# One odd product in 16 on VectorE, read-out two units behind, projection started one block earlier

## The chip, the cores and the metric

The kernel runs on one core of one Trainium2 chip. The metric is the device time of one execution in microseconds (us); before the change it is 21,916.79 us, the median of 3 runs (21,913.64 to 21,924.9). The engines are named as the profile names them: PE (TensorE), ACT (ScalarE), DVE (VectorE), POOL (GpSimd) and SP (SyncE, which issues the DMAs). PSUM is the accumulator memory, SBUF the working memory.

## What is computed

The input x is 16 images of 64 x 64 pixels with 96 channels, in fp32. Two residual layers follow each other. The first upsamples a group-normalised image, runs a small per-pixel network with a quadratic activation, filters and subsamples. The second, which the change is about, is a selective state-space scan over the pixels in four directions. Its core in the reference:

```python
delta = jax.nn.softplus(dts + dt_bias[None, :, :, None])
def step(h, inps):
    dt, ut, bt, ct = inps
    h = jnp.exp(dt[..., None] * As[None]) * h + (dt * ut)[..., None] * bt[:, :, None, :]
    y = jnp.einsum('bkdn,bkn->bkd', h, ct)
    return (h, y)
_, ys = jax.lax.scan(step, h0, (dT, uT, BT, CT))
...
y = ys[:, 0] + ys[:, 2, :, ::-1] + y_wh
...
y = out_norm_w * (y - mu) * jax.lax.rsqrt(var + EPS) + out_norm_b
y = y * z
```

There are 4,096 pixels in a sequence, 192 channels, 16 states per channel and 4 directions. For each channel and state the recurrence is h = decay * h + drive, with decay = exp(delta * A) and drive = delta * u * B; the result is the sum over states of h * C.

## The kernel before

**Tiling.** The scan is cut into 16 images x 8 steps. A step is 1,024 pixels (T) of one pair of directions: four steps forwards, then four backwards. A step has 6 blocks of two groups of 32 channels each, and a block has 4 units, each of which takes 4 of the 16 states of both groups: 32 channels x 4 states fill 128 partitions. So a step has 24 units, an image 192, and the whole run 3,072. The two groups of a unit are called e = 1 (here: odd) and e = 0 (even).

**One unit n** of the loop (the loop at L833), in the order in which it is issued:
- `recur(n, 1)`: DVE scans the odd group. It reads the decay `da` from PSUM and the drive `b` from SBUF and writes the states over `b` (L740 forwards, L742 backwards).
- `keep`: ACT copies the last column into the tile `new`, as the start of the next step (L748). The last step of a direction keeps nothing.
- `decay(n + 1, 1)`: ACT makes the odd decay of the next unit in PSUM (L725). There are two `da` buffers.
- `read_out(n - 1)`: PE multiplies the states times C of the unit before with `fold_s`, which sums over the 4 states, into the PSUM tile `y` (L764). One `y` tile serves the 4 units of a block; in backward steps it starts from the stored forward part `y0` (L757).
- POOL multiplies the odd states by `ct`, the rows of C, in place (L877), and then runs `drive(n + 2)`, the product of `dtu` and `bt` for both groups of the unit after next (L731). `b` has three buffers.
- `recur(n, 0)`: DVE scans the even group, over `da` in PSUM. DVE multiplies by `ct` from PSUM into `b` (L887), ACT keeps the last column and makes `decay(n + 1, 0)`.
- `store`: when a block's last read-out has been issued, ACT copies `y` out (L775) and a DMA writes it.

**Background work.** Between these, three places per unit (`slot(0)`, `slot(1)`, `slot(2)`; 72 positions a step) take one slice each of other work, written as Python generators that yield at each slice. `project` prepares the next step: it loads u (L634), projects it to `pp` on PE (L640), copies it to `pr` (L643), and for each of 3 channel groups v makes softplus: `s` on PE (L650), `e` and `d` on ACT (L658 to L661), `d` and `s` and `dtu` on DVE (L664 to L672), `delta` on ACT (L674); `dtu` and `delta` go to DRAM (L676, L677) and come back broadcast over partitions (L684). `front` makes the first layer and the convolution of the next image, `finish` the norm and output projection of the image before. A pace is kept: a generator advances while slices done / positions is below the ratio set for it (`SLICES` over 576 for front and finish, `PSLICES` over 59 for project).

**Order and queues.** The order on every engine is the order of issue above (a manual schedule); nothing reorders it. All DMAs go through SP's queue. Waits between engines are semaphores that the framework places from the tiles that are read, written and reused. At the start of a step's last block (unit 20) the projection of the next step is drained and its first `dtu` fetched.

Of the kernel before, what the change touches and what calls it, by code (L numbers as in the profile page):

```python
# [45 lines left out]
F32 = mybir.dt.float32  # L46
# [5 lines left out]
C = 96  # L52
# [19 lines left out]
SLICES = 540  # L72
WAIT = -1
HEAVY = 2
PSLICES = 60
# [3 lines left out]
def tile_two_blocks(  # L79
# [103 lines left out]
    b12 = ctx.enter_context(tc.tile_pool(name="b12", bufs=1))  # L183
# [56 lines left out]
    def front(mi):  # L240
# [72 lines left out]
        for p0 in range(0, UPS, PP):  # L313
# [94 lines left out]
        JS = 44  # L408
        s = [
            b18.tile([UPS, JS, C], F32, name="s0", tag="b18"), b12.tile([UPS, HW - JS, C], F32, name="s1", tag="b12")  # L410
        ]
        for _ in range(2):
            yield
        for i, n, first in [(0, JS // 4, k * JS // 4) for k in range(4)] + [(1, 10, 0), (1, 10, 10)]:
            nc.sync.dma_start(out=s[i][:, first:first + n, :], in_=s_d[:, JS * i + first:JS * i + first + n, :])
            yield
# [4 lines left out]
        for j0 in range(0, HW + 8, 8):  # L421
            if done is not None:
                nc.scalar.activation(
                    x1v[:, :, j0 - 8:j0], done.rearrange("c w h -> c h w"), AF.Identity, bias=shift
                )
            if j0 < HW:
# [5 lines left out]
                for j in range(8):  # L432
                    nc.tensor.matmul(
                        done[:, j, :], lhsT=s[(j0 + j) // JS][:, (j0 + j) % JS, :], rhs=down_s, start=False, stop=True,
                        skip_group_check=True,
                    )
            yield
        yield from parts(made["x1"], x1)
# [167 lines left out]
    def scan():  # L606


        with ExitStack() as es:
            pj = es.enter_context(tc.tile_pool(name="sc_pj", bufs=1))  # L610
            up_ = es.enter_context(tc.tile_pool(name="sc_u", bufs=3))
            cp = es.enter_context(tc.tile_pool(name="sc_bc", bufs=5))
            p3 = es.enter_context(tc.tile_pool(name="sc_3", bufs=3))
            p2 = es.enter_context(tc.tile_pool(name="sc_2", bufs=2))
            yp = es.enter_context(tc.tile_pool(name="sc_y", bufs=1))
            stp = es.enter_context(tc.tile_pool(name="sc_st", bufs=2))
            banks.append(es.enter_context(tc.tile_pool(name="b_ps", bufs=2, space=PSUM)))
# [4 lines left out]
            def project(mi, pair, lc, out):  # L622
# [3 lines left out]
                out["rows"] = rows = dram.tile([2, 2 * NS, T], F32, name="rows")  # L626
                out["delta"] = [dram.tile([128, T], F32, name=f"delta_d{v}") for v in range(3)]
                out["dtu"] = [dram.tile([128, T], F32, name=f"dtu_d{v}") for v in range(3)]
                xs_d = image[mi]["xs"]
                for t in range(0, T, TB):  # L630
                    u = []
                    for v in range(3):
                        uv = up_.tile([128, TB], F32, name="u")
                        nc.sync.dma_start(out=uv, in_=xs_d[v, :, lc * T + t:lc * T + t + TB])  # L634
                        u.append(uv)
                    for _ in range(3):
                        yield
# [3 lines left out]
                    yield  # L641
# [4 lines left out]
                    for i, v in enumerate((0, 2, 1)):  # L646
# [20 lines left out]
                        yield  # L667
# [60 lines left out]
            def drive(n):  # L728
                b = p3.tile([128, 2, T], F32, name="b")
# [14 lines left out]
            def keep(n, e, h):  # L744
                st, bi, j = units[n]
                if st % NT < NT - 1:
                    end = h[:, T - 1:T] if steps[st][1] == 0 else h[:, 0:1]
                    nc.scalar.copy(states[bi][1][:, e, j:j + 1], end)  # L748
# [77 lines left out]
            last = len(units) - 1  # L826
            for n in range(2):
                drive(n)
# [4 lines left out]
            for n, (st, bi, j) in enumerate(units):  # L833
# [184 lines left out]
```

## Time and profile before

| what | us |
|---|---|
| median of 3 runs | 21,916.79 |
| the profiled execution, its own time | 21,910.69 |
| its span, first to last instruction | 21,908.9 |
| first product on POOL starts | 513.35 |
| last product on POOL ends | 21,745.4 |
| DVE busy between 16,000 and 21,000 us | 4,695.32 of 5,000 |
| POOL busy between 16,000 and 21,000 us | 4,928.27 of 5,000 |

The profile lists, for each group of instructions, the source line, engine and operation, the tiles written and read with their shapes, a count, the busy time in us and the mean of one in ns; after a second bar, the time that the engine stood idle just before instructions of the group, and what ended it. A list of waits has, for each pair of lines, the total us, the number of times, and the longest. A timeline has the start and the duration in us, and in brackets the idle time before and its releaser. Durations of neighbours on one engine overlap by up to 0.1 us, so the step from start to start is the better measure of what an instruction costs.

### The profile page before, as it was taken

Reading aid. Unit: us, or ns where it says so; the run is one execution under the profiler, and the core shown is the slowest. Engines: PE = TensorE matmul, PEld = TensorE weight load, DVE = VectorE, ACT = ScalarE, POOL = GpSimd, SP = SyncE. Lnnn points to the kernel's source line nnn. Section 1 sums busy time; section 2 is a strip of 40 time slices with the busy share of each in tenths; the row PEclk is TensorE's granted clock in tenths of the full one; section 3 lists DMA queues with packets and bytes.
Section 4 is the critical chain, followed back from the end, with each engine's and each line's share of the span. In section 5 each row is a group of like instructions: output and inputs, shape, how many; then the busy total and the mean of one; then the engine's idle time right before and its main releaser. Section 6 shows DMA issues by size and latency. Waiting matters only on the chain.

```text
span 21908.9 us, 260666 instructions
## 1 busy us (share of the span) xinstructions
PE 15342.2 (70%) x92844; PEld 6324.7 (29%) x92844; DVE 19849.9 (91%) x12829; ACT 13130.2 (60%) x20854; POOL 20900.4 (95%) x6152
## 2 busy tenths in 40 slices
PE   6766767766777677777767677767777677677745
PEld 4322323232232322324233232322323223242211
DVE  0999999999999999999999999999999999999996
ACT  4665656666565665656656566665656656566543
POOL 0999999999999999999999999999999999999997
PEclk7776777877778777777877778777787877778856
DMA  2555565656656566565655656556565655656654
GB/s 80 190 191 188 193 214 194 209 195 200 205 191 215 189 206 201 192 215 192 207 198 194 214 192 209 196 201 206 193 211 189 210 199 198 206 195 208 210 177 134
DMA packets 1851895, 4276.30 MB, mean 195 GB/s; under 512 B 449118, under 2 KB 548350, under 8 KB 1848542
## 3 DMA queue, kind: packets, MB, share of 16 engines
q1 hardware_dynamic: 1850590, 4259.62, 58.1%
q8 instruction: 731, 11.98, 0.2%
q14 instruction: 574, 4.70, 0.1%
HBM read 3380.58 MB, written 878.18 MB: 194 GB/s over the span
## 4 chain that ended last, share of the span: by engine, by line
DVE 36%; POOL 19%; issue 18%; PE 9%; ACT 9%; DMA 7%; SPq 1%; POOLq 0%; DVEq 0%; ACTq 0%
POOL b L731 10%; POOL b L877 10%; DVE da L742 7%; DVE da L740 7%; DVE b L740 6%; DVE b L742 6%; DVE b L887 4%; ACT da L725 4%; DMA u<-xs_d 2%; DVE s L669 2%; DVE dtu L672 2%; DVE s L668 2%; PE y L764 1%; DMA ct<-rows 1%; PE pp L640 1%
## 5 line engine op out<-in xcount | busy, mean ns | idle before, releaser
L731 POOL TENSOR_TENSOR b<-dtu,bt 128x2048 f32<-128x2048 f32 x3072 | 13984.9, 4552 | 584.6 <-DMA dtu<-dtu_d 522.9
L725 ACT ACTIVATE da<-delta,a_s 128x1024 f32<-128x1024 f32 x6144 | 6853.5, 1116 | 2826.6 <-DVE b L887 1185.9
L877 POOL TENSOR_TENSOR b<-b,ct 128x1024 f32<-128x1024 f32 x3072 | 7309.1, 2379 | 259.8 <-ACT new L748 249.5
L764 PE MATMUL y<-b,fold_s 128*32 128x256 f32 x49152 | 4638.9, 492 | 4107.3 <-DVE b L887 3102.6
L887 DVE TENSOR_TENSOR b<-da,ct 128x1024 f32<-128x1024 f32 x3072 | 3752.6, 1222 | 84.5
L764 PEld LDWEIGHTS y<-b,fold_s 128*32 128x32 f32 x49152 | 1353.3, 126 | 7627.7 <-DVE b L887 4083.3
L740 DVE TENSOR_TENSOR_SCAN da<-da,new,b 128x1024 f32<-128x1024 f32 x1152 | 2694.3, 2339 | 252.3 <-ACT da L725 252.3
L740 DVE TENSOR_TENSOR_SCAN b<-da,new,b 128x1024 f32<-128x1024 f32 x1152 | 2698.0, 2342 | 174.1 <-POOL b L731 166.9
L742 DVE TENSOR_TENSOR_SCAN da<-da,new,b 128x1024 f32<-128x1024 f32 x1152 | 2693.8, 2338 | 172.9 <-ACT da L725 172.7
L742 DVE TENSOR_TENSOR_SCAN b<-da,new,b 128x1024 f32<-128x1024 f32 x1152 | 2697.1, 2341 | 151.6 <-POOL b L731 109.5
L748 ACT COPY new<-da 128x1 f32<-128x1 f32 x2304 | 362.3, 157 | 3028.5 <-DVE b L887 3023.2
L473 PE MATMUL c_ps<-xgp,wtap_s 96*128 96x512 f32 (+1 forms) x4608 | 1817.8, 675 | 168.9 <-ACT row L491 164.1
L650 PE MATMUL s<-pr,dtw_s 128*128 128x512 f32 x1536 | 1120.4, 819 | 557.8 <-ACT delta L674 516.7
L377 PE MATMUL o_ps<-w2c_s,hsq 128*100 128x96 f32 x9600 | 1205.3, 293 | 191.9 <-ACT hsq L348 180.1
L365 PE MATMUL h_ps<-xu,w1t_s 96*128 96x500 f32 x1920 | 1147.6, 700 | 244.2 <-ACT hsq L348 108.6
L748 ACT COPY new<-b 128x1 f32<-128x1 f32 x2304 | 432.6, 188 | 1445.7 <-DVE b L742 740.4
L377 PEld LDWEIGHTS o_ps<-w2c_s,hsq 128*100 128x100 f32 x9600 | 1119.5, 203 | 407.4 <-ACT hsq L348 227.7
L640 PE MATMUL pp<-u,xpt_s 128*128 128x512 f32 x1536 | 903.7, 734 | 224.2 <-DMA u<-xs_d 216.0
L742 DVE TENSOR_TENSOR_SCAN b<-da,b 128x1024 f32<-128x1024 f32 x384 | 876.7, 2283 | 133.2 <-ACT da L725 74.8
L473 PEld LDWEIGHTS c_ps<-xgp,wtap_s 96*128 96x128 f32 (+1 forms) x4608 | 631.9, 182 | 1193.3 <-issue 938.6
L740 DVE TENSOR_TENSOR_SCAN da<-da,b 128x1024 f32<-128x1024 f32 x384 | 875.8, 2281 | 106.9 <-ACT da L725 106.9
L742 DVE TENSOR_TENSOR_SCAN da<-da,b 128x1024 f32<-128x1024 f32 x384 | 876.0, 2281 | 105.0 <-ACT da L725 105.0
(120 smaller groups left out, 18077.1 us busy)
## 6 DMA issues: line engine op xcount, KB each, us to landing
dtu<-dtu_d SPq DMA_DIRECT2D x1536, 512.0 KB
delta<-delta_d SPq DMA_DIRECT2D x1536, 512.0 KB
bt<-rows SPq DMA_DIRECT2D x1024, 512.0 KB
ct<-rows SPq DMA_DIRECT2D x1024, 512.0 KB
u<-xs_d SPq DMA_DIRECT2D x896, 256.0 KB
dtu_d<-dtu SPq DMA_DIRECT2D x768, 256.0 KB
delta_d<-delta SPq DMA_DIRECT2D x768, 256.0 KB
xr<-in_x SPq DMA_DIRECT2D x768, 128.0 KB
```

Of the source, the lines that this page charges most:

```text
L365: nc.tensor.matmul(h_ps[j], lhsT=w1t_s[:, 128 * j:128 * (j + 1)], rhs=xu.rearrange("c p q -> c (p q)"), start=True, stop=True,)
L377: nc.tensor.matmul(o_ps[:, p, :], lhsT=hsq[j][:, UPS * p:UPS * (p + 1)], rhs=w2c_s[:, j, :], start=(j == 0), stop=(j == HB - 1),)
L473: nc.tensor.matmul(c_ps[p:p + n], lhsT=wtap_s[:, tap, 128 * i:128 * i + n], rhs=xgp[:, h0:h0 + 8, dx:dx + HW], start=(tap == 0), stop=(tap ...
L640: nc.tensor.matmul(pp, lhsT=xpt_s[:, pair, v, :], rhs=u[v], start=(v == 0), stop=(v == 2))
L650: nc.tensor.matmul(s, lhsT=dtw_s[:, pair, v, :], rhs=pr, start=True, stop=True)
L725: nc.scalar.activation(da, ops["delta", n // NQ][:, e, :], AF.Exp, scale=a_s[:, k, g, units[n][2]:units[n][2] + 1])
L731: nc.gpsimd.tensor_mul(b, ops["dtu", n // NQ], bt.unsqueeze(1).to_broadcast([128, 2, T]))
L740: nc.vector.tensor_tensor_scan(out, da, b, before, ALU.mult, ALU.add)
L742: nc.vector.tensor_tensor_scan(out[:, ::-1], da[:, ::-1], b[:, ::-1], before, ALU.mult, ALU.add)
L764: nc.tensor.matmul(y[32 * q:32 * q + 32, e, :], lhsT=fold_s, rhs=b[:, e, QT * q:QT * q + QT], start=(pair == 0 and j == 0 and e == 0), sto ...
L877: nc.gpsimd.tensor_mul(h, h, bc[1, r, j])
L887: nc.vector.tensor_mul(bs[n][:, 0, :], h, bc[1, r, j])
```

## The change

- Of every 16 units the last (n % 16 = 15) has its odd states written to PSUM, over `da`, and multiplied by `ct` on DVE instead of POOL. `keep` then copies from PSUM, after the product.
- `read_out` and `store` run two units behind instead of one. `b` has four buffers instead of three. `fetch_y0` is issued at the end of a block for the next one.
- The projection for step k is begun at the last block of step k - 2 (`next_step`) instead of at the start of step k - 1, and paced 71 slices over 72 positions instead of 60 over 59. Two positions instead of one lie after `pp`, after the second `s` on ACT and after `delta`. The first u tiles are fetched four slices ahead, the second ones as soon as a buffer is free (four u buffers instead of three). The DRAM tiles of a step have three buffers.
- In `front`, `s` is loaded into one buffer in two turns of 40 and 24 rows (before: two tiles, 44 and 20), with two slices between neighbouring groups of matmuls. `SLICES` goes from 540 to 550.

```diff
@@ -69,10 +69,11 @@
 NEPS = 1e-5
 BOTH = "natural_log_exp_and_others"
 POS = 3 * 8 * 6 * NQ
-SLICES = 540
+SLICES = 550
+SHARE = 16
 WAIT = -1
 HEAVY = 2
-PSLICES = 60
+PSLICES = 71
 
 
 @with_exitstack
...
@@ -405,14 +405,16 @@
         stow(sd, UPS - 2 * PG)
 
 
-        JS = 44
-        s = [
-            b18.tile([UPS, JS, C], F32, name="s0", tag="b18"), b12.tile([UPS, HW - JS, C], F32, name="s1", tag="b12")
-        ]
+        def fetch_s(first, n):
+            t = b18.tile([UPS, n, C], F32, name="s", tag="b18")
+            for k in range(0, n, 8):
+                nc.sync.dma_start(out=t[:, k:k + 8, :], in_=s_d[:, first + k:first + k + 8, :])
+                yield t, first
+
+        JS = 40
         for _ in range(2):
             yield
-        for i, n, first in [(0, JS // 4, k * JS // 4) for k in range(4)] + [(1, 10, 0), (1, 10, 10)]:
-            nc.sync.dma_start(out=s[i][:, first:first + n, :], in_=s_d[:, JS * i + first:JS * i + first + n, :])
+        for s, s_first in fetch_s(0, JS):
             yield
         yield
         x1 = xt
@@ -423,6 +425,11 @@
                 nc.scalar.activation(
                     x1v[:, :, j0 - 8:j0], done.rearrange("c w h -> c h w"), AF.Identity, bias=shift
                 )
+            if j0 == JS:
+                for s, s_first in fetch_s(JS, HW - JS):
+                    yield
+                for _ in range(2):
+                    yield
             if j0 < HW:
                 done = bank([C, 8, HW], "e_ps")
                 nc.tensor.matmul(
...
@@ -608,12 +617,13 @@
 
         with ExitStack() as es:
             pj = es.enter_context(tc.tile_pool(name="sc_pj", bufs=1))
-            up_ = es.enter_context(tc.tile_pool(name="sc_u", bufs=3))
+            up_ = es.enter_context(tc.tile_pool(name="sc_u", bufs=4))
             cp = es.enter_context(tc.tile_pool(name="sc_bc", bufs=5))
-            p3 = es.enter_context(tc.tile_pool(name="sc_3", bufs=3))
+            p4 = es.enter_context(tc.tile_pool(name="sc_4", bufs=4))
             p2 = es.enter_context(tc.tile_pool(name="sc_2", bufs=2))
             yp = es.enter_context(tc.tile_pool(name="sc_y", bufs=1))
             stp = es.enter_context(tc.tile_pool(name="sc_st", bufs=2))
+            dctx = es.enter_context(tc.tile_pool(name="dctx", bufs=3, space=bass.MemoryType.DRAM))
             banks.append(es.enter_context(tc.tile_pool(name="b_ps", bufs=2, space=PSUM)))
             aps = es.enter_context(tc.tile_pool(name="sc_aps", bufs=2, space=PSUM))
             yps = es.enter_context(tc.tile_pool(name="sc_yps", bufs=1, space=PSUM))
@@ -623,27 +633,32 @@
 
 
 
-                out["rows"] = rows = dram.tile([2, 2 * NS, T], F32, name="rows")
-                out["delta"] = [dram.tile([128, T], F32, name=f"delta_d{v}") for v in range(3)]
-                out["dtu"] = [dram.tile([128, T], F32, name=f"dtu_d{v}") for v in range(3)]
+                out["rows"] = rows = dctx.tile([2, 2 * NS, T], F32, name="rows")
+                out["delta"] = [dctx.tile([128, T], F32, name=f"delta_d{v}") for v in range(3)]
+                out["dtu"] = [dctx.tile([128, T], F32, name=f"dtu_d{v}") for v in range(3)]
                 xs_d = image[mi]["xs"]
+                order = (0, 2, 1)
+
+                def fetch_u(v, t):
+                    uv = up_.tile([128, TB], F32, name="u")
+                    nc.sync.dma_start(out=uv, in_=xs_d[v, :, lc * T + t:lc * T + t + TB])
+                    return uv
+
+                ahead_u = [fetch_u(v, 0) for v in order]
+                for _ in range(4):
+                    yield
                 for t in range(0, T, TB):
-                    u = []
-                    for v in range(3):
-                        uv = up_.tile([128, TB], F32, name="u")
-                        nc.sync.dma_start(out=uv, in_=xs_d[v, :, lc * T + t:lc * T + t + TB])
-                        u.append(uv)
-                    for _ in range(3):
-                        yield
+                    u, ahead_u = dict(zip(order, ahead_u)), []
                     pp = gps.tile([128, TB], F32, name="pp", tag="g")
                     for v in range(3):
                         nc.tensor.matmul(pp, lhsT=xpt_s[:, pair, v, :], rhs=u[v], start=(v == 0), stop=(v == 2))
-                    yield
+                    for _ in range(2):
+                        yield
                     pr = pj.tile([128, TB], F32, name="pr")
                     nc.scalar.activation(pr, pp, AF.Identity, bias=bumps_s)
 
 
-                    for i, v in enumerate((0, 2, 1)):
+                    for i, v in enumerate(order):
                         if i == 0:
                             yield
                         s = gps.tile([128, TB], F32, name="s", tag="g")
@@ -664,7 +679,8 @@
                         nc.vector.scalar_tensor_tensor(d, s, 0.0, d, ALU.max, ALU.add)
                         yield
                         nc.scalar.activation(s, e, AF.Identity, bias=one_s)
-                        yield
+                        for _ in range(2):
+                            yield
                         nc.vector.scalar_tensor_tensor(s, s, -1.0, e, ALU.add, ALU.subtract)
                         nc.vector.tensor_sub(s, d, s)
                         dtu = pj.tile([128, TB], F32, name="dtu")
@@ -672,19 +688,25 @@
                         nc.vector.tensor_mul(dtu, s, u[v])
                         yield
                         nc.scalar.copy(delta, s)
-                        yield
+                        for _ in range(2):
+                            yield
                         nc.sync.dma_start(out=out["dtu"][v][:, t:t + TB], in_=dtu)
                         nc.sync.dma_start(out=out["delta"][v][:, t:t + TB], in_=delta)
+                        if t + TB < T and i < 2:
+                            ahead_u += [fetch_u(k, t + TB) for k in (order[:1], order[1:])[i]]
+
+            def spread(out, what, ctx, bi, e):
+
+                v, s0, r = blocks[bi]
+                nc.sync.dma_start(
+                    out=out,
+                    in_=ctx[what][v][32 * (s0 + e):32 * (s0 + e) + 32, :].unsqueeze(1).to_broadcast([32, NQ, T]),
+                )
 
             def fetch(what, ctx, bi):
-
-                v, s0, r = blocks[bi]
                 t = p2.tile([128, 2, T], F32, name=what)
                 for e in (1, 0):
-                    nc.sync.dma_start(
-                        out=t[:, e, :],
-                        in_=ctx[what][v][32 * (s0 + e):32 * (s0 + e) + 32, :].unsqueeze(1).to_broadcast([32, NQ, T]),
-                    )
+                    spread(t[:, e, :], what, ctx, bi, e)
                 return t
 
             def fetch_bc(ctx, r, j, what):
@@ -726,7 +748,7 @@
                 das[n, e] = da
 
             def drive(n):
-                b = p3.tile([128, 2, T], F32, name="b")
+                b = p4.tile([128, 2, T], F32, name="b")
                 bt = bc[0, blocks[units[n][1]][2], units[n][2]]
                 nc.gpsimd.tensor_mul(b, ops["dtu", n // NQ], bt.unsqueeze(1).to_broadcast([128, 2, T]))
                 bs[n] = b
@@ -741,11 +763,11 @@
                 else:
                     nc.vector.tensor_tensor_scan(out[:, ::-1], da[:, ::-1], b[:, ::-1], before, ALU.mult, ALU.add)
 
-            def keep(n, e, h):
+            def keep(n, e, h, copy):
                 st, bi, j = units[n]
                 if st % NT < NT - 1:
                     end = h[:, T - 1:T] if steps[st][1] == 0 else h[:, 0:1]
-                    nc.scalar.copy(states[bi][1][:, e, j:j + 1], end)
+                    copy(states[bi][1][:, e, j:j + 1], end)
 
             def read_out(n):
                 st, bi, j = units[n]
@@ -824,6 +846,15 @@
                 (ahead_gen if ahead_gen.gen is not None else behind_gen).slot(position)
 
             last = len(units) - 1
+            def next_step(st, mi):
+
+                nonlocal step_gen
+                if st < len(steps):
+                    if steps[st][0] > mi:
+                        ahead_gen.drain()
+                    step_gen = Background(project(*steps[st], ctxs[st]), PSLICES, 3 * per_step)
+
+            next_step(1, 0)
             for n in range(2):
                 drive(n)
             for e in range(2):
@@ -843,10 +874,6 @@
                 elif n % per_image == 2 and mi > 0:
                     behind_gen = Background(finish(mi - 1), SLICES, POS)
                 if j == 0:
-                    if bi == 0 and st + 1 < len(steps):
-                        if steps[st + 1][0] > mi:
-                            ahead_gen.drain()
-                        step_gen = Background(project(*steps[st + 1], ctxs[st + 1]), PSLICES, 59)
                     new = stp.tile([128, 2, NQ], F32, name="new", tag=f"st{bi}")
                     states[bi] = (states[bi][1] if states[bi] else None, new)
 
@@ -857,41 +884,46 @@
                     elif n + NQ <= last:
                         step_gen.drain()
                         ahead = ctxs[st + 1], 0
+                        next_step(st + 2, mi)
                     if ahead:
                         ops["dtu", m + 1] = fetch("dtu", *ahead)
                 elif j == 1:
                     if ahead:
                         ops["delta", m + 1] = fetch("delta", *ahead)
-                    if n + NQ <= last and steps[units[n + NQ - 1][0]][1] == 1:
-                        st2, bi2, _ = units[n + NQ - 1]
-                        y0s[steps[st2][2], bi2] = fetch_y0(steps[st2][2], bi2)
-
-                h = bs[n][:, 1, :]
+
+                odd_here = n % SHARE == SHARE - 1
+                h = das[n, 1] if odd_here else bs[n][:, 1, :]
                 recur(n, 1, h)
-                keep(n, 1, h)
+                if odd_here:
+                    nc.vector.tensor_mul(bs[n][:, 1, :], h, bc[1, r, j])
+                keep(n, 1, h, nc.scalar.copy)
                 if n < last:
                     decay(n + 1, 1)
-                if n:
-                    read_out(n - 1)
+                if n >= 2:
+                    read_out(n - 2)
                 slot(0)
-                nc.gpsimd.tensor_mul(h, h, bc[1, r, j])
+                if not odd_here:
+                    nc.gpsimd.tensor_mul(h, h, bc[1, r, j])
                 if n + 2 <= last:
                     drive(n + 2)
 
                 h = das[n, 0]
                 recur(n, 0, h)
-                if n and units[n - 1][2] == NQ - 1:
-                    storing = store(n - 1)
+                if n >= 2 and units[n - 2][2] == NQ - 1:
+                    storing = store(n - 2)
                     next(storing)
                 slot(1)
                 nc.vector.tensor_mul(bs[n][:, 0, :], h, bc[1, r, j])
-                keep(n, 0, h)
+                keep(n, 0, h, nc.scalar.copy)
                 if n < last:
                     decay(n + 1, 0)
                 slot(2)
                 if storing is not None:
                     next(storing, 0)
                     storing = None
+                if j == NQ - 1 and n < last and steps[units[n + 1][0]][1] == 1:
+                    st2, bi2, _ = units[n + 1]
+                    y0s[steps[st2][2], bi2] = fetch_y0(steps[st2][2], bi2)
 
 
                 at = n % per_step
...
```

More of the change, by code (lines that the diff above doesn't have):

```diff
@@ L182, in tile_two_blocks @@
     b18 = ctx.enter_context(tc.tile_pool(name="b18", bufs=1))
-    b12 = ctx.enter_context(tc.tile_pool(name="b12", bufs=1))
     b2p = ctx.enter_context(tc.tile_pool(name="b2", bufs=11))
@@ L433, in front @@
                     nc.tensor.matmul(
-                        done[:, j, :], lhsT=s[(j0 + j) // JS][:, (j0 + j) % JS, :], rhs=down_s, start=False, stop=True,
+                        done[:, j, :], lhsT=s[:, j0 + j - s_first, :], rhs=down_s, start=False, stop=True,
                         skip_group_check=True,
@@ L437, in front @@
             yield
+            if j0 < HW:
+                yield
         yield from parts(made["x1"], x1)
@@ L674, in project @@
                         nc.scalar.copy(delta, s)
-                        yield
+                        for _ in range(2):
+                            yield
                         nc.sync.dma_start(out=out["dtu"][v][:, t:t + TB], in_=dtu)
                         nc.sync.dma_start(out=out["delta"][v][:, t:t + TB], in_=delta)
+                        if t + TB < T and i < 2:
[6 more added lines that the diff above has]
+                )
             def fetch(what, ctx, bi):
-                v, s0, r = blocks[bi]
                 t = p2.tile([128, 2, T], F32, name=what)
                 for e in (1, 0):
-                    nc.sync.dma_start(
-                        out=t[:, e, :],
-                        in_=ctx[what][v][32 * (s0 + e):32 * (s0 + e) + 32, :].unsqueeze(1).to_broadcast([32, NQ, T]),
-                    )
+                    spread(t[:, e, :], what, ctx, bi, e)
                 return t
@@ L904, in scan @@
                         bc[what, 0, ahead_j] = fetch_bc(ctxs[st + 1], 0, ahead_j, what)
-            read_out(last)
+            for n in (last - 1, last):
+                read_out(n)
             for _ in store(last):
```

## The prediction

> **What bounds the kernel now.** I read the page's busy times first, then the groups, then each engine's waits, then a timeline of one unit of work. A unit is one pass of the scan loop; there are 3,072.
>
> ```profile
> PE 15342.2 (70%) x92844; PEld 6324.7 (29%) x92844; DVE 19849.9 (91%) x12829; ACT 13130.2 (60%) x20854; POOL 20900.4 (95%) x6152
> L731 POOL TENSOR_TENSOR b<-dtu,bt 128x2048 f32<-128x2048 f32 x3072 | 13984.9, 4552 | 584.6 <-DMA dtu<-dtu_d 522.9
> L877 POOL TENSOR_TENSOR b<-b,ct 128x1024 f32<-128x1024 f32 x3072 | 7309.1, 2379 | 259.8 <-ACT new L748 249.5
> L887 DVE TENSOR_TENSOR b<-da,ct 128x1024 f32<-128x1024 f32 x3072 | 3752.6, 1222 | 84.5
> ```
>
> GpSimd's only work is two rows, and VectorE is close behind. GpSimd's waits say how full it is:
>
> ```profile
> POOL b L731 <- DMA dtu<-dtu_d: 522.9, 9, 512.3
> POOL b L877 <- ACT new L748: 249.5, 168, 4.0
> POOL b L731 <- PE y L764: 15.9, 17, 2.5
> ```
>
> One wait of 512.3 is the prologue: GpSimd's first product starts at 513.35 us and its last ends at 21,745.4. So the scan stage takes 21,232 us, with 164 us of tail after it (span 21,908.9). Inside it GpSimd idles 584.6 - 512.3 + 259.8 = 332 us, 1.6%. Now the same for VectorE and ScalarE:
>
> ```profile
> DVE da L740 <- ACT da L725: 359.2, 285, 5.9
> DVE da L742 <- ACT da L725: 277.6, 267, 2.4
> DVE d L664 <- ACT d L661: 250.6, 36, 128.1
> DVE b L740 <- POOL b L731: 216.8, 270, 1.1
> DVE b L742 <- POOL b L731: 166.5, 198, 1.1
> DVE b L742 <- ACT da L725: 114.8, 90, 1.5
> ...
> ACT pr L643 <- PE pp L640: 444.8, 171, 14.0
> ```
>
> VectorE waits on GpSimd for 216.8 + 166.5 = 383 us. On ScalarE's decays it waits 757 us in the scan stage (the da and b rows, with a small b L740 row, less one wait of 22 before it), and about 148 us more in the projection (L664, L668 and smaller rows, without the prologue's 128). The three together are 1,288 of its idle time; some 140 us are hand-over gaps. Without GpSimd, VectorE with ScalarE behind it would thus need 21,232 - 383 = 20,849 us; GpSimd alone needs 20,900. **Two chains of equal length, coupled by a small buffer, cost 332 us more than the longer one.** That reading carries the rest. One unit shows both:
>
> ```profile
> 11527.20 2.35 POOL L877 TENSOR_TENSOR b<-b,ct 128x1024 f32<-128x1024 f32 x1
> 11529.52 4.52 POOL L731 TENSOR_TENSOR b<-dtu,bt 128x2048 f32<-128x2048 f32 x1
> 11534.01 2.34 POOL L877 TENSOR_TENSOR b<-b,ct 128x1024 f32<-128x1024 f32 x1
> ...
> 11527.09 1.23 DVE L887 TENSOR_TENSOR b<-da,ct 128x1024 f32<-128x1024 f32 x1
> 11528.23 2.34 DVE L740 TENSOR_TENSOR_SCAN b<-da,new,b 128x1024 f32<-128x1024 f32 x1
> 11531.76 2.36 DVE L740 TENSOR_TENSOR_SCAN da<-da,new,b 128x1024 f32<-128x1024 f32 x1 [1.19 <-ACT da L725]
> ...
> 11528.35 0.16 ACT L748 COPY new<-da 128x1 f32<-128x1 f32 x1
> 11530.61 1.12 ACT L725 ACTIVATE da<-delta,a_s 128x1024 f32<-128x1024 f32 x1 [2.10 <-DVE b L740]
> ```
>
> Start to start GpSimd takes 2.32 + 4.49 = 6.81 us a unit. The even decay at 11,530.61 could have followed the copy at 11,528.35. It waits for the odd scan to end (11,530.57) instead, though it reads nothing of it, and VectorE then stands for 1.19 us. In the instruction lists with their semaphores such a decay carries a VectorE wait and the copy L748 behind it a GpSimd wait: a wait that belongs to the copy has been put one instruction early. The list of before has 515 such places; matched by unit, they hold 532 of the 638 us that even scans wait for a decay, and hardly any other unit waits. I call these **early waits**.
>
> **The Trainium skill.** *SBUF — State Buffer*, "SBUF: two separate sides": VectorE and GpSimd share a port pair as an exclusive lock, taken by a VectorE operation with two SBUF inputs. The added product reads one input from PSUM, as L887 does; beside all present VectorE work L877 keeps 2.33 to 2.73 us, so I add nothing for contention. *GPSIMD Engine Reference*, 4.1, calls a two-input product about twice as slow there as on VectorE; the trace agrees (2,379 against 1,222 ns). *Perfetto Trace Analysis*, "Identifying Dependency Chains", says that an instruction with several waits may have them put ahead of it; L725 carries 1,172 separate semaphore instructions here, in agreement.
>
> **The change, part by part.**
>
> *Odd product of every 16th unit.* 3,072 / 16 = 192 products leave GpSimd: 192 x 2.32 = 445 us, so GpSimd alone needs 20,900 - 445 = 20,455. VectorE gets 192 of L887's form: 1.14 us start to start (11,527.09 to 11,528.23). The odd scan then writes PSUM and the product must await it, as scan to L887 does now (about 2.36 us against 2.26 between two scans): +0.10. Together 192 x 1.24 = 238 us. Behind it on VectorE stands the even scan, later by 1.24. The odd decay of the next unit waits for the product to free its PSUM tile; its scan comes later by as much, so nothing. Each such unit shifts the two engines by 2.32 + 1.24 = 3.6 us. GpSimd's leeway between the end of an odd scan and the next unit's odd scan is about 5.8 - 2.5 = 3.3 us (a unit without projection, less scan and copy). So GpSimd will sometimes run dry just after. The 15 units until the next shift rebuild its backlog where VectorE's unit (about 6.5 us with projection) is below 6.81.
>
> *Early waits.* The list of the changed kernel has 268 places instead of 515. In 134 the stretch between the two scans is empty: 134 x 1.19 = 159; in 104 the first projection operation lies there and covers half: 104 x 0.6 = 62; the others about 15. That is 237 against 532: -295 us on VectorE. It is the largest term I found that the diff doesn't mention, and it also lets the state copy, hence GpSimd, go earlier (61 of the 168 waits on the copy stand at early waits, 77 of 249.5 us).
>
> *Read-out one pair later, four b buffers.* TensorE no longer stops for the product just made. It frees at most the 15.9 us of GpSimd waits on y. TensorE, 70% busy, is otherwise off the path, and the moved read-out, y store and y0 fetch keep their order on SP and TensorE. I take 0, bounds 0 to -16.
>
> *Projection.* Its 58 slices in 59 positions become 71 in 72 and begin at the last block of the step before: four units sooner, ended at the same unit. VectorE's projection work, some 16 us a step, no longer leaves units 20 to 2 free; 365 of 468 VectorE waits on GpSimd fall in units 20 to 3, where VectorE is light. Two positions between dependent operations and inputs fetched ahead attack ScalarE's 444.8 us on pp and VectorE's 148 us on L664 and the like. ScalarE is 60% busy, so only the second counts: between 0 and -148, I take -80. All DMAs of a step move with it: three input fetches, the row stores and the dtu and delta stores pass SP sooner. dtu and delta are wanted at the same unit as before and v=0 is stored first; three DRAM contexts let two projections overlap. 0, bounds 0 to +50.
>
> *Front part.* Loading s in two turns of one buffer puts 3 DMAs behind the first 40 rows' matmuls: in the prologue some +5 us; later behind the five positions that it leaves free. ScalarE copies stay.
>
> **Sum.** VectorE with ScalarE: 20,849 + 238 - 295 - 80 = 20,712. GpSimd: 20,455. VectorE becomes the longer by 257 us. On top come its waits on GpSimd: 383 now; halved to 190, as the light units are broken up and GpSimd is the shorter chain. Scan stage 20,902 against 21,232: -330, and +5: **-325 us**, 21,584 in span. The profiled execution (21,910.69) lies 6 us under the median; from 21,916.79 the forecast is **21,592**.
>
> **Rivals.**
> 1. *GpSimd stays the bound* (0.20). For: 95% busy, its sum is exact. Against: VectorE's 20,712. If VectorE's ScalarE waits fall further (by 300), 445 us come off and half of the copy waits (125): 21,347 to 21,472, say 21,410.
> 2. *The coupling stays whole* (0.20). For: a 3.6 us shift against 3.3 of leeway. VectorE's 20,712 plus today's 332: 21,044, -188: 21,730.
> 3. *VectorE takes over with its stalls kept: slower* (0.11). For: it is 91% busy, and 905 us of its idle time are ScalarE's, not GpSimd's. If the early waits merely turn into late ScalarE elsewhere, VectorE needs 20,849 + 238 = 21,087, plus 190 to 383 of GpSimd waits: 21,277 to 21,470, that is +45 to +238; about 21,990. It decides once VectorE's waits on ScalarE fall by less than 45 us. Against: early waits are fixed in the list, 247 fewer.
> 4. *The pieces cancel* (0.04): as 3, with 45 to 100 us of stalls gone, 21,917.
>
> **How the numbers follow.** The forecast has 0.45: with the unknown terms' ends (-148 or 0 for the projection, +50 for DMAs, 120 to 260 for the coupling) it runs from 21,450 to 21,720. To hold 8 in 10 the range goes from 21,410 to 21,800. Faster by over 0.2% (44 us, about what this measurement can tell): 0.45 + 0.20 + 0.20 = 0.85; within: 0.04; slower: 0.11.
>
> **What would show it.** GpSimd near 20,455 busy, with 2,880 products beside scans and 192 gone; 192 new VectorE products of about 1,222 ns; even-scan waits on decays of 1.19 us near halved, 638 to about 350; VectorE's waits on GpSimd near 190; GpSimd's idle time in the scan stage up from 332 to about 450. I am wrong if the even-scan waits stay near 638 (rival 3), if VectorE's waits on GpSimd exceed its waits on ScalarE with GpSimd idle under 300 (rival 1), or if a DMA heads GpSimd's waits.

## The result and the profile after

The changed kernel takes 21,746.1 us (median of 4 runs, 21,740.9 to 21,747.8); the kernel before, run beside it, 21,915.2. The ratio is 0.9922, interval 0.9905 to 0.9939: **169 us faster**, about half of the 325 us that were forecast, and 154 us above the forecast time. The page after, and below it the new products from the list of all groups:

```profile
PE 15137.2 (70%) x92844; PEld 6450.9 (30%) x92844; DVE 20237.7 (93%) x13021; ACT 13127.2 (60%) x20854; POOL 20459.0 (94%) x5960
...
L753 POOL TENSOR_TENSOR b<-dtu,bt 128x2048 f32<-128x2048 f32 x3072 | 13908.9, 4531 | 528.8 <-DMA dtu<-dtu_d 514.9
...
L906 POOL TENSOR_TENSOR b<-b,ct 128x1024 f32<-128x1024 f32 x2880 | 6801.7, 2362 | 589.8 <-ACT new L770 564.3
...
L916 DVE TENSOR_TENSOR b<-da,ct 128x1024 f32<-128x1024 f32 x3072 | 3753.2, 1222 | 84.5
...
L898 DVE TENSOR_TENSOR b<-da,ct 128x1024 f32<-128x1024 f32 x192 | 235.2, 1225 | 18.4 <-DVE da L762 0.5
```

L753 is the old L731, L906 the old L877, L916 the old L887. GpSimd has lost 192 products and 441 us, and stands at 20,459 where 20,455 was forecast. But VectorE's busy time grew by 20,237.7 - 19,849.9 = 388 us, and the 192 new products (L898, 1,225 ns each) explain only 235 of it. **Some 150 us of VectorE's busy time are unaccounted for, about as much as the forecast is off.** The scan stage lasts from 516.0 to 21,578.1, 21,062 us, where 20,902 was forecast; the prologue grew by 2.6 us and the tail by 4, so the loss lies in the stage. The waits (in all, times, longest, us) of GpSimd:

```profile
POOL b L906 <- ACT new L770: 564.3, 325, 10.5
POOL b L753 <- DMA dtu<-dtu_d: 514.9, 1, 514.9
...
POOL b L753 <- PE y L786: 12.4, 21, 1.4
```

And of VectorE:

```profile
DVE nb L236 <- ACT rg L233: 335.4, 16, 279.4
DVE d L679 <- ACT d L676: 160.2, 8, 127.6
DVE da L762 <- ACT da L747: 158.2, 167, 1.3
DVE b L762 <- POOL b L753: 123.2, 162, 1.1
DVE b L764 <- POOL b L753: 106.3, 130, 1.1
DVE b L764 <- ACT da L747: 105.4, 60, 4.0
DVE da L764 <- ACT da L747: 103.4, 118, 1.5
```

The even scans' waits for a decay (`da` L762 and L764, before L740 and L742) have gone from 637 to 262 us (23 of them at the odd scans that now write `da`). The `d` wait has gone from 250.6 to 160.2, of which only 4.5 lie in the scan stage, where there were 89.5. GpSimd now waits 564 us for the state copy, with single waits of up to 10.5 us where 4.0 was the longest. A wait of 10 us is more than a whole unit. The timeline at one of them (start, duration, engine, line, operation):

```profile
3801.43 4.50 POOL L753 TENSOR_TENSOR b<-dtu,bt 128x2048 f32<-128x2048 f32 x1
...
3803.83 1.23 DVE L916 TENSOR_TENSOR b<-da,ct 128x1024 f32<-128x1024 f32 x1
...
3804.97 12.20 DVE L236 TENSOR_TENSOR nb<-nmean,rg 96x1 f32<-96x1 f32 x1
...
3805.89 2.35 POOL L906 TENSOR_TENSOR b<-b,ct 128x1024 f32<-128x1024 f32 x1
...
3808.21 8.94 POOL L753 TENSOR_TENSOR b<-dtu,bt 128x2048 f32<-128x2048 f32 x2
...
3817.09 2.34 DVE L762 TENSOR_TENSOR_SCAN da<-da,new,b 128x1024 f32<-128x1024 f32 x1
...
3820.80 1.12 ACT L747 ACTIVATE da<-delta,a_s 128x1024 f32<-128x1024 f32 x1 [13.42 <-DVE b L898]
```

L236 multiplies two columns of 96 numbers, for the norm of the next image's `front`. It is one element per partition, and is recorded as 12.2 us of VectorE. It ends when GpSimd has finished the product it was in and three more, and has nothing left to do. The next scan, its copy, and GpSimd's next products all come behind it. The tile view of `nb` (duration in ns: least, median, most; first and last start) shows that the line itself is old and only its duration is new. Before:

```profile
L236 DVE TENSOR_TENSOR nb<-nmean,rg x32: 155/499/1320, 38.8 to 19752.2; 96x1 f32<-96x1 f32 x32
```

After:

```profile
L236 DVE TENSOR_TENSOR nb<-nmean,rg x32: 154/5139/12217, 39.5 to 19622.1; 96x1 f32<-96x1 f32 x32
```

`front` has two norms, at units 6 and 94 of an image. The second one's `nb` is the long one: 15 times about 12 us; the first one's takes 0.15 us, but for a single 10.1. Before, the second stood at unit 92, between the even scan and its product. It has moved with `front`, to which the change adds slices ahead of this norm while it raises `SLICES`: with the odd product alone (experiment 4) it is still at unit 92, with the old projection at 94. By the starts of the odd scans, averaged over the 15 images that have a next one, step 3 (units 72 to 95) grew from 166.4 to 173.4 us, where the other steps grew by 1.4 at most or shrank by up to 7.7.

The suspect has a mechanism in the Trainium skill, *SBUF — State Buffer*, "SBUF: two separate sides": a VectorE operation with two SBUF inputs and a GpSimd operation that reads SBUF exclude each other on one port pair, and whichever starts first keeps it for its whole instruction. `nmean` and `rg` both lie in SBUF, and the trace agrees that VectorE is shut out: each of the 16 long `nb` ends within 0.02 us of the end of a GpSimd product. What it does not follow is the span: here one VectorE instruction waits through the ends of three GpSimd instructions without getting in.

### The profile page after: what moved, and what is told of

Same layout as the page of the kernel before. It is cut to its first block, busy times and chain, and to the rows that moved or that the text cites. A ratio compares the mean times of both kernels' runs of the same rounds, so it can differ in the third digit from the quotient of the medians.

```text
span 21746.0 us, 260144 instructions
## 1 busy us (share of the span) xinstructions
PE 15137.2 (70%) x92844; PEld 6450.9 (30%) x92844; DVE 20237.7 (93%) x13021; ACT 13127.2 (60%) x20854; POOL 20459.0 (94%) x5960
## 5 line engine op out<-in xcount | busy, mean ns | idle before, releaser
L753 POOL TENSOR_TENSOR b<-dtu,bt 128x2048 f32<-128x2048 f32 x3072 | 13908.9, 4531 | 528.8 <-DMA dtu<-dtu_d 514.9
L906 POOL TENSOR_TENSOR b<-b,ct 128x1024 f32<-128x1024 f32 x2880 | 6801.7, 2362 | 589.8 <-ACT new L770 564.3
L786 PE MATMUL y<-b,fold_s 128*32 128x256 f32 x49152 | 4298.2, 479 | 1336.0 <-DVE b L916 853.9
L916 DVE TENSOR_TENSOR b<-da,ct 128x1024 f32<-128x1024 f32 x3072 | 3753.2, 1222 | 84.5
L762 DVE TENSOR_TENSOR_SCAN da<-da,new,b 128x1024 f32<-128x1024 f32 x1232 | 2880.5, 2338 | 114.7 <-ACT da L747 87.5
L764 DVE TENSOR_TENSOR_SCAN da<-da,new,b 128x1024 f32<-128x1024 f32 x1232 | 2879.6, 2337 | 70.6 <-ACT da L747 48.6
L786 PEld LDWEIGHTS y<-b,fold_s 128*32 128x32 f32 x49152 | 1482.6, 128 | 4466.8 <-issue 1465.9
L762 DVE TENSOR_TENSOR_SCAN b<-da,new,b 128x1024 f32<-128x1024 f32 x1072 | 2511.3, 2343 | 115.7 <-POOL b L753 106.7
L764 DVE TENSOR_TENSOR_SCAN b<-da,new,b 128x1024 f32<-128x1024 f32 x1072 | 2509.6, 2341 | 91.5 <-POOL b L753 71.5
L665 PE MATMUL s<-pr,dtw_s 128*128 128x512 f32 x1536 | 1193.3, 869 | 1619.4 <-ACT delta L690 1229.0
L482 PE MATMUL c_ps<-xgp,wtap_s 96*128 96x512 f32 (+1 forms) x4608 | 1738.2, 652 | 396.3 <-ACT row L500 391.8
L654 PE MATMUL pp<-u,xpt_s 128*128 128x512 f32 x1536 | 1046.5, 827 | 633.3 <-ACT delta L690 376.9
L762 DVE TENSOR_TENSOR_SCAN da<-da,b 128x1024 f32<-128x1024 f32 x400 | 911.8, 2279 | 70.7 <-ACT da L747 70.7
L764 DVE TENSOR_TENSOR_SCAN da<-da,b 128x1024 f32<-128x1024 f32 x400 | 911.6, 2279 | 55.3 <-ACT da L747 54.8
L764 DVE TENSOR_TENSOR_SCAN b<-da,b 128x1024 f32<-128x1024 f32 x368 | 840.0, 2283 | 126.7 <-ACT da L747 88.1
```

Of the source, the lines that this page charges most:

```text
L482: nc.tensor.matmul(c_ps[p:p + n], lhsT=wtap_s[:, tap, 128 * i:128 * i + n], rhs=xgp[:, h0:h0 + 8, dx:dx + HW], start=(tap == 0), stop=(tap ...
L654: nc.tensor.matmul(pp, lhsT=xpt_s[:, pair, v, :], rhs=u[v], start=(v == 0), stop=(v == 2))
L665: nc.tensor.matmul(s, lhsT=dtw_s[:, pair, v, :], rhs=pr, start=True, stop=True)
L753: nc.gpsimd.tensor_mul(b, ops["dtu", n // NQ], bt.unsqueeze(1).to_broadcast([128, 2, T]))
L762: nc.vector.tensor_tensor_scan(out, da, b, before, ALU.mult, ALU.add)
L764: nc.vector.tensor_tensor_scan(out[:, ::-1], da[:, ::-1], b[:, ::-1], before, ALU.mult, ALU.add)
```

## The experiments

Theory P (port): the lost time is `nb`, shut out by GpSimd through its two SBUF inputs. The rival: `nb` only shows a stop that has another cause (its input, or the new coupling of the two chains, which the forecast had put at 190 us of waits on GpSimd).

**1. The same product in a form with one SBUF tensor**, the other as the scalar of each partition:

```diff
-        nc.vector.tensor_mul(nb, nmean, rg)
+        nc.vector.tensor_scalar(nb, nmean, rg, None, ALU.mult)
```

> The changed kernel with one instruction in another form: nb = nmean * rg in norm as a tensor_scalar with rg as a per-partition scalar (one SBUF tensor input) instead of a product of two SBUF tensors. Port theory: the 12.2 us that this 96x1 product takes at unit 94 of an image is VectorE shut out of SBUF by GpSimd; it falls to about 0.2 us, VectorE's busy time by some 170 to 190 us, and the time from 21,746 by 150 to 190 us to about 21,575. Rival, the stall only stands where VectorE would have waited for GpSimd anyway: nb gets short and the time stays within 40 us of 21,746.

> The kernel before with the same edit of nb. There nb took 0.5 and 1.3 us a time, 27 us in 32 executions. Port theory: at most 25 us come off, 21,895 to 21,917. Rival, the form of the instruction is worth something in itself (a shorter norm, earlier slices): 100 us or more come off here too.

Measured: on the changed kernel **21,579.8 us**, ratio to before 0.9849 (0.9834 to 0.9863), 166 us faster than the change as it was. On the kernel before, the same edit gives 21,917.0, ratio 1.0002 (0.9993 to 1.0011): nothing. The tile view, then the timeline at the same place, of the changed kernel with the edit:

```profile
L236 DVE TENSOR_SCALAR nb<-nmean,rg x32: 200/208/211, 40.1 to 19467.7; 96x1 f32<-96x1 f32 x32
```

```profile
3779.03 1.22 DVE L916 TENSOR_TENSOR b<-da,ct 128x1024 f32<-128x1024 f32 x1
3780.17 0.20 DVE L236 TENSOR_SCALAR nb<-nmean,rg 96x1 f32<-96x1 f32 x1
```

Same place behind the product, same input, 0.20 us instead of 12.20. P holds as far as the form of the input goes. In the scan stage all `nb` together took 195 us and now take 6, so 189 us were to be had (VectorE's busy time falls from 20,237.7 to 20,056.2), and 166 came. GpSimd's waits for the copy fall from 564 to 390 us, and step 3 of an image from 173.4 to 162.2. That the memory of the inputs counts, and not the kind of instruction, experiment 5 shows at another line, where the instruction stays the same. The port itself is the page's explanation; the runs show who waits for whom.

**2. Why did it pass in the kernel before?** Two theories. A: the drive that GpSimd starts there used to wait for GpSimd's own last product, and that let VectorE in; with the read-out two units behind and four `b` buffers this wait is gone. B: the missing odd product leaves GpSimd in another phase. Each is undone alone on the changed kernel, with `nb` as the change has it. For A (`store` goes back with the read-out):

```diff
-            p4 = es.enter_context(tc.tile_pool(name="sc_4", bufs=4))
+            p4 = es.enter_context(tc.tile_pool(name="sc_4", bufs=3))
...
-                if n >= 2:
-                    read_out(n - 2)
+                if n:
+                    read_out(n - 1)
```

> The changed kernel with the read-out one unit behind and three b buffers again. In its instruction list GpSimd's drives again wait for GpSimd's own last product (2,878 of 3,072, against 191 in the changed kernel), and there are 319 early waits instead of 268. Theory A, the own wait is what let VectorE in between two GpSimd instructions: nb at unit 94 falls to 1.3 us or less, about 170 us come off and some 50 to 60 go back for the early waits: about 21,630. Theory B, nb is shut out because the odd product of unit 95 is missing on GpSimd: nb stays at about 12 us and the time rises to about 21,800.

For B, `SHARE = 16` became `1 << 20`, so that no product moves to VectorE:

> The changed kernel with every odd product on GpSimd, as before; all else as in the change (299 early waits, no drive waits for GpSimd's own product). GpSimd busy 20,900, scan products 3,072. Theory A: nb stays long (8 us or more). Theory B: nb is 1.3 us or less. Time: GpSimd is the bound, 20,900 plus 200 to 350 us of idle in the scan stage: 21,780 to 21,930. If the product on VectorE brought nothing, the time would be below 21,746.

Measured: 21,840.3 (0.9968, 0.9955 to 0.9981) and 21,804.0 (0.9951, 0.9936 to 0.9966). The tile view of `nb` without the lag:

```profile
L236 DVE TENSOR_TENSOR nb<-nmean,rg x32: 155/6118/12225, 39.5 to 19707.0; 96x1 f32<-96x1 f32 x32
```

And with all odd products on GpSimd:

```profile
L236 DVE TENSOR_TENSOR nb<-nmean,rg x32: 155/7614/10107, 39.0 to 19668.1; 96x1 f32<-96x1 f32 x32
```

`nb` stays long in both, so neither alone is the cause: **A and B both fall.** The first run shows something else, though. Read-out one unit behind with three buffers costs 94 us against the change as it was. GpSimd's waits for the copy rise to 631 us, those of the even scans to 358. Of the 94 us some 28 lie at `nb` itself, which takes 2.1 us at the first norm instead of 0.15 (223 us in the scan stage against 195).

**3. Is it the place?** Three yields in place of one ahead of L236 put `nb` two positions later, where it again stands between an even scan and its product, as before the change:

```diff
-        yield
+        for _ in range(3):
+            yield
         nc.vector.tensor_mul(nb, nmean, rg)
```

> The changed kernel with two more positions ahead of nb = nmean * rg, still a product of two SBUF tensors. The second norm's nb then stands between the even scan and the product of unit 96, as in the kernel before (unit 92), no longer behind the product of unit 94. Place theory: where it meets GpSimd's stream decides, it takes 1.3 us or less there, and 120 to 170 us come off: about 21,600. Rival, GpSimd's stream leaves no opening anywhere now: it takes 7 us or more there too, and the time stays within 50 us of 21,746.

Measured: 21,699.6 (0.9902, 0.9888 to 0.9917), between the change and experiment 1, 46 us better than the change. The tile view:

```profile
L237 DVE TENSOR_TENSOR nb<-nmean,rg x32: 155/5134/6664, 39.5 to 19593.0; 96x1 f32<-96x1 f32 x32
```

The longest is 6.7 us instead of 12.2, and all of them take 157 us in the scan stage instead of 195. The place counts, but it is not the whole of it, since the kernel before passed in 1.3 us at most. One last run joined the two: one unit's lag, three buffers, the later place, and the odd product moved to `n % 16 == 7`, so that the drive there again waits for GpSimd's own last product.

> The kernel with the read-out one unit behind and three b buffers, nb two positions later (between the even scan and the product of unit 96), still a product of two SBUF tensors, and the odd product on VectorE at n % 16 = 7. There GpSimd's drive behind the product of unit 96 waits for GpSimd's own last product again, as in the kernel before; in the run with nb later alone it does not, and nb took 5.9 us. If that own wait lets VectorE in, nb takes 1.3 us or less at unit 96; if it does not matter, about 5.9. It is a look at nb; the time, 21,720 to 21,850, tells nothing on it.

Its `nb` at that place took 9.1 us (10.7 at the other norm; longest of all 11.1), and the one execution took 21,782. Here a wait of GpSimd's own did not let VectorE in. What decides it stays open. No run has the two-input `nb` beside the old projection, so the new projection as a cause is untested.

**4. What each part is worth.** The odd product alone, put on the kernel before:

> The kernel before with the odd product of every 16th unit on VectorE and nothing else of the change. 449 early waits instead of 515. By the sum: GpSimd 20,455, VectorE with ScalarE 20,849 + 238 - 75 = 21,010, plus 190 to 330 of waits on GpSimd, plus 677 outside the scan stage: 21,880 to 22,020, no gain alone. Rival, GpSimd is the bound even so: 150 us or more below the kernel before, 21,760 or less.

Measured: 21,924.7, ratio 1.0004 (0.9996 to 1.0013). GpSimd has its 430 us less (busy 20,470) and none of it arrives. VectorE has 208 us more to do (busy 20,057), its even scans still wait 597 us for decays, and GpSimd now waits 513 us for copies instead of 250:

```profile
POOL b L882 <- ACT new L749: 513.0, 416, 4.8
...
DVE da L741 <- ACT da L726: 317.5, 236, 4.9
...
DVE da L743 <- ACT da L726: 279.1, 263, 2.4
```

Next the kernel of experiment 1 with one part undone: all odd products on GpSimd, or the old projection (58 slices, begun at unit 0, one position between neighbours, u fetched on demand):

> The run with nb in the pointer form (21,580), with all odd products on GpSimd. GpSimd busy 20,890, and it is the longer chain: plus 150 to 250 of idle and 680 outside, 21,720 to 21,820. So the product on VectorE is worth 140 to 240 us once the projection is spread. Rival, the projection's new places alone made the gain: 21,580 to 21,640.

> The run with nb in the pointer form (21,580), with the projection as before (begun at the step's start, 60 slices over 59 positions, one position between neighbours, u fetched on demand). 433 early waits instead of 268. Early-wait theory: some 165 x 1.05 = 175 us of waits of even scans come back, and up to 125 of waits on d and s: 21,780 to 21,900, with even-scan waits on ScalarE of about 430 us instead of 268. Rival, the projection's place is hidden: within 60 us of 21,580.

Measured: 21,699.0 (0.9899, 0.9883 to 0.9916), so the odd product is worth 119 us there; and 21,781.1 (0.994, 0.9925 to 0.9955), so the new projection, its places and its fetches ahead taken together, is worth 201. The waits of VectorE with the old projection:

```profile
DVE da L753 <- ACT da L738: 263.6, 245, 2.8
DVE da L755 <- ACT da L738: 246.3, 232, 2.8
DVE d L674 <- ACT d L671: 237.5, 51, 127.6
```

And with the new one:

```profile
DVE da L762 <- ACT da L747: 164.8, 172, 1.4
DVE d L679 <- ACT d L676: 161.8, 8, 127.8
...
DVE da L764 <- ACT da L747: 103.4, 118, 1.5
```

The even scans' waits are 510 against 268 us. Most of what was called the early waits goes with the projection: the list has 433 of them with the old projection, 268 with the new.

**5. A second line of this kind, and the ratio.** `lin` (96x96, two SBUF tensors, once an image) took 3.0 us at the median. With ScalarE writing its input to PSUM only one SBUF tensor is left:

```diff
-        nc.scalar.activation(lin, mt_s, AF.Identity, scale=rg)
+        lin_ps = bank([C, C], "lin_ps")
+        nc.scalar.activation(lin_ps, mt_s, AF.Identity, scale=rg)
...
-        nc.vector.tensor_add(lin, lin, ident_s[0:C, 0:C])
+        nc.vector.tensor_add(lin, lin_ps, ident_s[0:C, 0:C])
```

> The run with nb in the pointer form (21,580), and lin = lin + ident read from PSUM too, so that the image's other small product of two SBUF tensors has one SBUF input. That sum takes 2.96 us there; about 0.25 us alone. Port theory: up to 16 x 2.7 = 43 us off, 21,535 to 21,580. Rival, it stands where VectorE would wait anyway: 21,575 to 21,590. Faster than the kernel before and the changed one either way.

Measured: 21,547.0 (0.9832, 0.9817 to 0.9846), 33 us less than with `nb` alone. The tile view after the change and then with the edit:

```profile
L259 DVE TENSOR_TENSOR lin<-lin,ident_s x16: 245/3014/3020, 40.3 to 19030.3; 96x96 f32<-96x96 f32 x16
```

```profile
L260 DVE TENSOR_TENSOR lin<-lin_ps,ident_s x16: 241/243/245, 40.3 to 18841.2; 96x96 f32<-96x96 f32 x16
```

Both are a TENSOR_TENSOR of the same shape; what differs is that one input lies in PSUM. Here too the order of the work around it counts: without any edit of its own `lin` took 1.3 us in the kernel before, and 0.24 in the run of experiment 2 with all odd products on GpSimd.

On top of both, one odd product in 12, then one in 24:

> As the run with nb and lin mended, one odd product in 12 on VectorE instead of 16: 64 more. GpSimd 20,310 busy, VectorE 79 us more, early waits 267. If VectorE's chain is the longer, as its sum says: 0 to +80 us against the run with nb and lin. If GpSimd is: -80 to -150.

> As the run with nb and lin mended, one odd product in 24 on VectorE: 64 fewer. GpSimd 20,605 busy, VectorE 79 us less, early waits 283. If VectorE's chain is much the longer: -40 to -80 us. If the two are level: -20 to +60. If GpSimd is the longer: +80 to +150.

Measured: **21,518.2 (21,517.3 to 21,521.4; 0.9819, 0.9803 to 0.9835)**, the fastest of all, 228 us below the change; and 21,536.2 (0.9827, 0.9812 to 0.9841). Both lie below the 21,547 of one in 16, by 29 and 11 us (the four runs of one in 16 spread over 10): near the best ratio the time does not follow the ratio in one direction.

## Why the prediction was right in direction and twice too large

**The step that failed** is the one on contention: "beside all present VectorE work L877 keeps 2.33 to 2.73 us, so I add nothing for contention". It looked for contention in GpSimd's durations, but here it is VectorE that is shut out, and it asked only of the added product, not of old lines that the change moves. `front` was costed by its DMAs ("ScalarE copies stay"); that its slices put `nb` in a new place was not looked at. The missing term is 166 us (experiment 1), and with it gone the kernel takes 21,580, 12 us under the forecast of 21,592.

That closeness is partly luck, as its terms show. In the kernel of experiment 1:
- *Odd product*: 235 us of new products on VectorE where 238 were forecast with the hand-over; GpSimd 20,458 busy against 20,455. Right.
- *Early waits*: forecast -295. All waits on decays in the scan stage went from 757 to 382 us, -375 (after: -381). Too small by 80. The list of 268 places was about right: in the trace, 267 even decays start at the end of the odd scan (480 before), and the even scans behind them wait 217 us where the forecast left 237. But the waits elsewhere, which the forecast left alone, fell too, from 127 to 29.
- *Projection*: forecast -80 within 0 to -148. VectorE's waits on ScalarE's `d`, `s` and copies in the scan stage went from 134 to 9 us, -125. (The forecast's 148 held one more wait of the prologue, 13.6 us.) In the range, taken too low by 45. As a cause the projection is worth more, since experiment 4 shows that the early waits go with it; the two terms are one edit.
- *Waits on GpSimd*: forecast 190. They were 282 (279 in the change). Too low by 92.

With these, 20,849 + 238 - 375 - 125 + 282 = 20,869 us for the scan stage; it lasted from 519.4 to 21,413.3, 20,894. The forecast had no term for VectorE's waits on `rg`, the input of `nb`: 36 us in the stage, none before. With it the sum is 20,905, 11 us too high, and these 11 were not taken apart. Errors of +92 and +36 were nearly cancelled by -80 and -45.

The forecast's own span was also added up wrongly: with all three upper ends that it names it reaches 21,592 + 80 + 50 + 70 = 21,792, not 21,720.

*Read-out and four buffers*: "I take 0, bounds 0 to -16". It was priced by the waits of GpSimd on `y` (15.9 us, now 12.4), which is right as far as it goes. The run without it is 94 us slower, but this does not refute the term: 28 us are at `nb`, and its list has 319 early waits instead of 268, whose price the forecast held under the early waits. In the trace 318 even decays start at the end of the odd scan instead of 270, and the waits behind them are 295 us instead of 221, 74 more. So this part of the change is worth more than its term, through waits that were counted elsewhere; what it is worth by itself stays open, and so does whether the lag or the buffers do it.

**The sum with one long chain** held as a reading: "two chains of equal length, coupled". The odd product alone gives nothing, and 119 us with the rest of the change and the short `nb`. The parts can't be added from single undoings, since each is worth what the others leave of it. Rival 2 (the coupling stays whole, 21,730) came nearest in time and for the wrong reason: VectorE's waits on GpSimd fell from 383 to 279 us. Rival 1 fell with VectorE's waits on decays still at 376 us. Rival 3, slower, fell at the point it named: VectorE's waits on ScalarE in the stage fell from 913 to 443 us, far more than 45. GpSimd's idle time in the stage rose to 604 us rather than 450, through `nb`: in the kernel of experiment 1 it is 437.

What stays open: at which of its instruction ends GpSimd gives way. In the changed kernels `nb` ended with the end of a GpSimd instruction, most often one after which it had nothing ready; in the kernel before, with the first. A wait of GpSimd's own and the missing odd product are excluded as the sole cause, and the place among VectorE's work counts. The remaining 268 early waits were not attacked by any run.

## What to carry to other kernels

When slices of background work are added or re-paced, look up where every old instruction lands, also one of a single element, and give those with two SBUF inputs that land beside a full GpSimd another form (a column as scalar, or an input in PSUM) before the change is judged. Read contention on the engine that can lose, by the longest duration of a line rather than its mean: 16 instructions in 13,021 took away half of what this change could gain. Here an engine relieved of work gained nothing while the waits of its partner stayed, so price such an edit in the kernel that has the other edits.

## What the runs showed of the hardware that was not expected

- A VectorE product of 96x1 with two SBUF inputs, 0.15 us at its shortest, stood for up to 12.2 us while GpSimd ran products back to back; in the kernel before it passed in 1.3 at most. The same product with one input as per-partition scalar took 0.20 to 0.21 us in the same place.
- The stop is booked as VectorE's busy time, not as a wait, so the views of waits do not name it: they show only ScalarE's 13.42 us and GpSimd's copy waits of up to 10.5 us behind it.
- A 96x96 sum with two SBUF inputs took 3.0 us in the changed kernel, and 0.24 with one of them in PSUM.
